# The third and fourth product of each slice change places in a fast-matrix-product attention kernel

## The chip, the cores and the metric

The kernel runs on one core of one Trainium2 chip. The metric is device microseconds of one execution. The median of the shown runs of the kernel before is 2908.41 us.

## The reference

The input `x` holds 128 graphs of 128 nodes with 768 features, and `adj` one 128x128 matrix for each graph. One pre-normalised attention layer with 12 heads of 64 is computed:

```python
h = relu(layernorm(x))                       # over the 768 features, eps 1e-5
q, k, v = split_heads(h @ Wq + bq), split_heads(h @ Wk + bk), split_heads(h @ Wv + bv)
scores = q @ k^T / sqrt(64) + beta * adj     # adj is shared by the 12 heads
scores = where(adj > 0, scores, -9e15)
out = x + merge_heads(softmax(scores) @ v)
```

The biases of the three projections are zero in the inputs, and everything is float32.

## The kernel before

**Tiling.** Four graphs make one group, and there are 32 groups (`G`). The features lie on the partitions, in three pairs of 128-row blocks. The projections of a group are done in three slices: `qk0` (queries and keys of heads 0 to 5), `v` (all values), `qk1` (queries and keys of heads 6 to 11). Seen in blocks, each slice is a 2x3 by 3x3 matrix product. It is computed with 15 block products instead of 18, each of a sum of blocks of the activations (names A.. and S..) with a sum of blocks of the weights (names B.. and T..). The table `PRODUCTS` holds them in the order in which they are issued. The first `qk0` slice, of group 0, is done plainly with 18 products, so 95 slices go by the table. The last slice of all has an order of its own, `LAST`, which is a list of positions in the table.

**Banks.** Each row of the table names a chain, a to d. The products of one chain are added up in one PSUM bank, one after another. After each product the running sum in the bank is added to, or taken from, the output blocks that the row lists: the first time that an output block is met it is written (by ScalarE in the qk slices, line 352, by VectorE in the v slices, line 342), and later it is updated by VectorE (line 356 or 347). This reading of a bank is called its drain here. The next product of the chain may write the bank only when its drain has ended. A chain takes a bank from the list of free ones at its first product and gives it back after its last:

```python
first = n == mine[0]
if first:
    banks[chain] = take()
```

There are eight banks, and the list is first in, first out.

**Scores.** With `SC_AT = 1`, the scores of six heads follow the second product of a slice, in the 31 `qk0` slices of groups 1 to 31, the 31 `v` slices of the same groups and the `qk1` slice of group 0. They take six banks at once, three pairs in the order `3u, 3u+2, 3u+1`:

```python
ps = {(oc, i): take() for oc in order for i in range(2)}
...
e = es[G, oc, i] = work.tile(...)
taken[0] = nc.vector.scalar_tensor_tensor(e, ps[oc, i]..., SCORE_CAP * ISCALE, biasT[G], ...)   # L381
give(ps[oc, i])
nc.scalar.activation(e, e, AF.Exp, scale=1.0 / ISCALE)                                          # L384
```

With the two banks that chains c and a hold by then, all eight are in use. The next bank that anybody takes is the one that the first line 381 has read. Line 377 is the matmul of the scores, line 410 that of probabilities with values (after products 5, 8 and 11), line 331 that of the block products. `issue_after(added[G].ins)` in `transposes` keeps the transposes for the next group (line 279, in `to_hT`) behind the latest VectorE drain traced so far. `HT_AT` places them after products 0 to 4 and 9 of the `qk1` slice. `stats` (line 227) reads the `x` tiles that `load_x` (line 152) brings in for a later group.

**Order of the work.** The Tile scheduler puts the instructions of each engine in an order at compile time, by the order of the program and by when it reckons each to be ready. VectorE, ScalarE and the DMA queue of SyncE then run their lists in that order.

Of the kernel before, what the change touches and what calls it, by code (L numbers as in the profile page):

```python
# [31 lines left out]
def kernel(  # L32
# [33 lines left out]
PRODUCTS = (  # L66
    ("S9", "T9", "c", (((1, 1), -1),)),
    ("A10", "T12", "a", (((1, 0), -1),)),
    ("S10", "T10", "b", (((1, 0), 1),)),
    ("S2", "T2", "c", (((0, 1), -1),)),  # L70
    ("S8", "B12", "d", (((1, 1), -1), ((1, 2), 1))),
    ("S6", "T6", "a", (((0, 0), -1),)),
    ("S3", "B01", "c", (((0, 2), -1),)),
# [694 lines left out]
```

## Time and profile before

| what | value |
| --- | --- |
| median of 5 runs | 2908.41 us (2906.64 to 2909.24) |
| the profiled execution's own time | 2904.81 us |
| its span | 2903.0 us |
| PE busy | 2878.8 us, 99% of the span |
| weight loads (PEld) busy | 2015.1 us, 69% |
| VectorE (DVE) busy | 1988.1 us, 68% |
| ScalarE (ACT) busy | 806.9 us, 28% |
| GpSimd (POOL) busy | 376.0 us, 13% |
| granted TensorE clock | 0.999 of full speed |

A line of a timeline gives the start and the length in us, the engine, the source line, the operation, what it writes and reads, and how many instructions were merged. At its end stand, in brackets, the idle time of the engine just before it and what ended that idle time. The weights of a product are loaded by PEld just ahead of its matmuls, so a wait of a product shows in front of its first weight load.

### The profile page before, as it was taken

How to read it: one execution, taken by the hardware profiler on the slowest of the kernel's cores; microseconds unless marked ns; L12 is line 12 of the kernel's file. 1: busy time of each engine (PE TensorE's matmuls, PEld its weight loads, DVE VectorE, ACT ScalarE, POOL GpSimd, SP SyncE). 2: the span in 40 equal slices, each digit the busy share in tenths (PEclk: the TensorE clock that was granted, in tenths of full speed). 3: DMA queues.
4: the chain of work that ended last, by engine and by line, in shares of the span. 5: the costliest groups of instructions: out<-in, count | busy, mean ns of one | idle time of the engine just before them, and what ended most of it. 6: DMA issues, size and time to landing. Idle time of an engine off the chain costs nothing.

```text
span 2903.0 us, 81884 instructions
## 1 busy us (share of the span) xinstructions
PE 2878.8 (99%) x35526; PEld 2015.1 (69%) x35526; DVE 1988.1 (68%) x5143; ACT 806.9 (28%) x1751; POOL 376.0 (13%) x307
## 2 busy tenths in 40 slices
PE   8999999999999999999999999999999999999998
PEld 6666777666667666766667666677666676666766
DVE  7876667666676666767667776667666677666765
ACT  2432322223222222223232232322223222322221
POOL 1111111111111111111111111111111111111110
PEclk9999999999999999999999999999999999999999
DMA  6312122221222111221112212122221222111211
GB/s 165 78 52 57 44 61 70 56 60 41 56 70 63 53 45 52 71 67 51 54 44 67 71 52 58 43 61 70 56 60 42 56 70 63 52 49 45 67 42 38
DMA packets 358622, 172.22 MB, mean 59 GB/s; under 512 B 84464, under 2 KB 358128, under 8 KB 358256
## 3 DMA queue, kind: packets, MB, share of 16 engines
q1 hardware_dynamic: 355392, 166.14, 21.2%
q8 instruction: 280, 4.59, 0.7%
q10 hardware_dynamic: 2864, 0.79, 0.1%
q14 instruction: 86, 0.70, 0.1%
HBM read 116.53 MB, written 50.33 MB: 57 GB/s over the span
## 4 chain that ended last, share of the span: by engine, by line
PE 83%; issue 8%; DVE 5%; POOL 2%; DMA 2%; SPq 1%; ACT 0%; ACTq 0%; POOLq 0%; DVEq 0%
PE bank L331 71%; PE bank L377 5%; PE bank L410 5%; DMA x<-in_x_dram 2%; PE bank L481 1%; DVE S L285 1%; POOL rstd L261 1%; POOL xo L415 1%; DVE qk L356 1%; DVE st L227 1%; DVE A L279 1%; SPq L152 0%; DVE o L393 0%; DVE e L381 0%; SPq L416 0%
## 5 line engine op out<-in xcount | busy, mean ns | idle before, releaser
L331 PE MATMUL bank<-S,qk_T 128*64 128x256 f32 x7056 | 822.6, 380 | 5.1 <-DVE e L381 3.1
L331 PEld LDWEIGHTS bank<-S,qk_T 128*64 128x64 f32 x7056 | 502.4, 137 | 263.8 <-DVE e L381 8.2
L356 DVE TENSOR_TENSOR qk<-qk,bank 128x512 f32<-128x512 f32 x630 | 430.1, 683 | 343.1 <-PE bank L331 342.9
L352 ACT ACTIVATE qk<-bank,bqk 128x256 f32<-128x256 f32 x756 | 313.4, 471 | 990.8 <-PE bank L331 848.3
L331 PE MATMUL bank<-S,qk_B 128*64 128x256 f32 x4032 | 478.3, 379 | 1.1 <-DVE qk L356 0.9
L331 PE MATMUL bank<-A,qk_T 128*64 128x256 f32 x4032 | 478.5, 379 | 0.4 <-DVE qk L356 0.4
L415 POOL TENSOR_TENSOR xo<-xo,o 128x512 f32<-128x512 f32 x189 | 256.1, 1355 | 1604.6 <-DVE o L393 993.1
L331 PE MATMUL bank<-v_T,S 128*64 128x256 f32 x3584 | 422.7, 380 | 0.0
L384 ACT ACTIVATE e<-e 128x512 f32<-128x512 f32 x378 | 227.6, 631 | 665.6 <-DVE e L381 664.8
L347 DVE TENSOR_TENSOR v<-v,bank 128x512 f32<-128x512 f32 x320 | 220.1, 688 | 264.8 <-PE bank L331 264.7
L331 PEld LDWEIGHTS bank<-A,qk_T 128*64 128x64 f32 x4032 | 283.6, 137 | 137.6 <-DVE qk L356 0.5
L331 PEld LDWEIGHTS bank<-S,qk_B 128*64 128x64 f32 x4032 | 277.9, 137 | 129.8 <-DVE qk L356 1.7
L331 PEld LDWEIGHTS bank<-v_T,S 128*64 128x64 f32 x3584 | 252.1, 137 | 126.5 <-issue 5.7
L272 ACT ACTIVATE x<-x,shift,rstd 128x192 f32<-128x192 f32 x512 | 228.1, 534 | 343.8 <-POOL shift L263 343.8
L331 PE MATMUL bank<-v_B,S 128*64 128x256 f32 x2048 | 244.7, 380 | 0.0
L381 DVE SCALAR_TENSOR_TENSOR e<-bank,biasT 128x512 f32<-128x512 f32 x378 | 231.4, 682 | 16.7 <-PE bank L377 16.7
L331 PE MATMUL bank<-v_T,A 128*64 128x256 f32 x2048 | 238.3, 379 | 0.0
L342 DVE TENSOR_TENSOR v<-bv_b,bank 128x512 f32<-128x512 f32 x192 | 131.9, 687 | 146.4 <-PE bank L331 146.4
L410 PEld LDWEIGHTS bank<-v,e 128*64 128x64 f32 x6048 | 208.5, 138 | 27.4
L279 DVE STREAM_TRANSPOSE A<-x 128x256 f32<-128x256 f32 x384 | 215.8, 614 | 7.6 <-ACT x L272 7.4
L227 DVE BATCH_NORM_STATS2 st<-x 128x6 f32<-128x192 f32 x512 | 160.9, 349 | 74.7 <-DMA x<-in_x_dram 74.2
L410 PE MATMUL bank<-v,e 128*64 128x65 f32 x6048 | 208.2, 221 | 0.0
(80 smaller groups left out, 1729.9 us busy)
## 6 DMA issues: line engine op xcount, KB each, us to landing
x<-in_x_dram SPq DMA_DIRECT2D x504, 96.0 KB, 2.5
xo<-in_x_dram SPq DMA_DIRECT2D x189, 256.0 KB, 2.8
out_dram<-xo SPq DMA_DIRECT2D x189, 256.0 KB, 2.2
adj<-in_adj_dram SPq DMA_DIRECT2D x128, 64.0 KB, 2.4
qk_T<-in_L_gnn_Wq_dram SPq DMA_DIRECT2D x10, 128.0 KB, 3.4
qk_T<-in_L_gnn_Wk_dram SPq DMA_DIRECT2D x10, 128.0 KB, 3.3
v_T<-in_L_gnn_Wv_dram SPq DMA_DIRECT2D x5, 256.0 KB, 5.9
qk_B<-in_L_gnn_Wq_dram SPq DMA_DIRECT2D x8, 128.0 KB, 3.4
```

The source lines that it names most:

```text
L227: nc.vector.bn_stats(st[G][:, g * NB + b, :], xg[G, g][:, b, :])
L272: nc.scalar.activation(t, t, AF.Relu, bias=shift[G, n], scale=rstd[G, n])
L279: last = nc.vector.transpose(t[:, :, g * N:(g + 1) * N].rearrange("p c (b i) -> p c b i", i=SQ), src)
L331: nc.tensor.matmul(p[q:q + HD, i, :], lhs[:, q:q + HD], rhs, start=(first and i == 0 and c == 0), stop=(c == 1), skip_group_check=True)
L347: added[G] = nc.vector.tensor_tensor(o, o, got, ALU.add if sign > 0 else ALU.subtract)
L352: nc.scalar.activation(t[:, i, :], p[:, i, :], AF.Identity, bias=bqk[:, i, oc:oc + 1], scale=float(sign))
L356: added[G] = nc.vector.tensor_tensor(t, t, p, ALU.add if sign > 0 else ALU.subtract)
L377: nc.tensor.matmul(ps[oc, i][k:k + HD, g * N:(g + 1) * N], t[r, 1, at][:, k:k + HD], t[r, 0, at], start=True, stop=True)
L381: taken[0] = nc.vector.scalar_tensor_tensor(e, ps[oc, i].rearrange("p (g n) -> p g n", g=GRP), SCORE_CAP * ISCALE, biasT[G], op0=ALU.min, ...
L384: nc.scalar.activation(e, e, AF.Exp, scale=1.0 / ISCALE)
L410: nc.tensor.matmul(pa[q:q + HD, 2 * g + i, :], es[G, oc, i][:, 2 * r + g, q:q + HD], vt[G, "v", r, h // 4][:, 4 * g + h % 4, :], start=Tru ...
L415: nc.gpsimd.tensor_add(t, t, o.rearrange("p a (b j) d -> p (a b) (j d)", j=2))
```

## The change

Two neighbouring rows of the table change places. Product S2·T2 of chain c now comes third, straight behind the scores where there are any, and product S10·T10, which opens chain b, comes fourth. All 95 slices that use the table are affected, also those without scores, and so is `LAST`, since it names positions. No instruction is added or removed.

```diff
     ("S9", "T9", "c", (((1, 1), -1),)),
     ("A10", "T12", "a", (((1, 0), -1),)),
+    ("S2", "T2", "c", (((0, 1), -1),)),
     ("S10", "T10", "b", (((1, 0), 1),)),
-    ("S2", "T2", "c", (((0, 1), -1),)),
     ("S8", "B12", "d", (((1, 1), -1), ((1, 2), 1))),
     ("S6", "T6", "a", (((0, 0), -1),)),
     ("S3", "B01", "c", (((0, 2), -1),)),
```

## The prediction

> **What bounds the kernel now.** I read the page first. PE is busy for 99% of the span, so only PE's pauses can be won, and only work on PE or a new pause can be lost.
>
> ```profile
> PE 2878.8 (99%) x35526; PEld 2015.1 (69%) x35526; DVE 1988.1 (68%) x5143; ACT 806.9 (28%) x1751; POOL 376.0 (13%) x307
> ```
>
> Second, the waits, asked for all engines; these three rows are the pauses in front of the weight loads of block products (us in total, times, longest):
>
> ```profile
> PEld bank L331 <- DVE e L381: 8.2, 22, 1.1
> PEld bank L331 <- issue: 7.7, 44, 0.3
> PEld bank L331 <- DVE qk L356: 6.5, 10, 1.4
> ```
>
> The first row is what the change aims at: the product behind the scores waits until line 381 has read a bank of the scores. It stands 22 times, for 8.2 us in all.
>
> Third, the timeline of PEld, to see how much of these 8.2 us is really a wait. A quiet place (a v slice) and a disturbed one (the qk0 slice with the longest wait):
>
> ```profile
> 233.88 2.61 PEld L377 LDWEIGHTS bank<-qk 64*64 64x64 f32 x96 [0.39 <-issue]
> 236.66 3.22 PEld L331 LDWEIGHTS bank<-v_T,S 128*64 128x64 f32 x32 [0.17 <-issue]
> ...
> 828.98 2.61 PEld L377 LDWEIGHTS bank<-qk 64*64 64x64 f32 x96 [0.38 <-issue]
> 832.69 3.22 PEld L331 LDWEIGHTS bank<-S,qk_T 128*64 128x64 f32 x32 [1.09 <-DVE e L381]
> ```
>
> A gap of 0.17 us follows the scores in every slice, also where nothing is waited for. It stays. What can go is 1.09 - 0.17 = 0.92 us in the worst slice. The `x32` shows that S10 and S2, 16 records each, follow the scores at once.
>
> Fourth, why line 381 is late there, from VectorE's timeline:
>
> ```profile
> 827.92 0.35 DVE L227 BATCH_NORM_STATS2 st<-x 128x6 f32<-128x192 f32 x1
> 830.91 1.14 DVE L227 BATCH_NORM_STATS2 st<-x 128x6 f32<-128x192 f32 x4 [2.63 <-DMA x<-in_x_dram]
> 831.96 3.66 DVE L381 SCALAR_TENSOR_TENSOR e<-bank,biasT 128x512 f32<-128x512 f32 x6
> ```
>
> VectorE stands in its queue for 2.63 us at statistics of a later group whose `x` has not landed, and line 381 is behind them.
>
> **The change part by part.**
>
> *The wait behind the scores goes.* S2 adds to chain c's bank, which no score holds. Subtracting the 0.17 us from each of the 22 gaps: 8.2 - 22 x 0.17 = 4.46 us. All 22 lie in qk0 slices. The 31 v slices, and the qk1 slice of group 0, show only the 0.17 us. S10 comes one product later, which is 1.73 us (weight loads of successive products start at 169.28, 171.01 and 172.73 us). The longest excess was 0.92 us, so S10 finds its bank free with 0.8 us to spare. S8 takes the second bank of the scores, which is read 0.61 us (3.66/6) after the first and asked for 3.45 us after S2: free too. Against the profiled execution's own time: 2904.81 - 4.46 = 2900.35 us.
>
> *What more a usual run holds.* The profiled execution took 2904.81 us, 1.81 us more than its span, and is 3.60 us below the median. From one scores stage of the qk0 slices to the next a period is 89.40 us where nothing is disturbed (2176.43 to 2265.83 us). The 30 periods from 115.13 to 2803.67 us sum to 2688.54 us, that is 6.54 us above 30 x 89.40. Nearly all of the 4.46 us is in this, the rest is mostly the third wait row. What varies within an execution is thus waits on late `x`, 4.46/6.54 = 0.68 of them of the kind that goes. Whether the 3.60 us are more of the same no view shows. The bounds are 0 and 3.60 us; I take the share, 0.68 x 3.60 = 2.45 us, since these waits are the nearest thing in the trace that varies. Sum: 4.46 + 2.45 = 6.9 us.
>
> *Chain c is entered again after one product instead of two.* Where scores stand between (62 slices and one more), 2.78 us of them lie between A10 and S2, so c is long drained. In 32 slices, nearly all qk1, nothing lies between but A10. The same place in ScalarE's and PEld's timelines:
>
> ```profile
> 171.44 0.84 ACT L352 ACTIVATE qk<-bank,bqk 128x256 f32<-128x256 f32 x2 [4.22 <-PE bank L331]
> ```
>
> ```profile
> 169.28 1.66 PEld L331 LDWEIGHTS bank<-S,qk_T 128*64 128x64 f32 x16
> 171.01 1.65 PEld L331 LDWEIGHTS bank<-A,qk_T 128*64 128x64 f32 x16
> 172.73 3.38 PEld L331 LDWEIGHTS bank<-S,qk_T 128*64 128x64 f32 x32
> ```
>
> S9 is drained from 171.44 to 172.28 us; the third product's first load starts at 172.73. So 0.45 us are left over, and A10 is the cover. ScalarE had been idle for some 4 us before that drain in every qk1 slice of groups 1 to 30, so this does not scatter. The v slice of group 0 has a VectorE drain there (49.44 to 50.13 us, with the third product due near 50.7), also in time. Cost 0. From above it is bounded by a drain wholly in the open, 0.88 us (0.84 and 0.04 of start) x 32 = 28 us; a gain is excluded, since chain c waits nowhere there today.
>
> The Trainium skill speaks against this step: Perfetto Trace Analysis, section Optimizing Tensor Performance, Matmuls, says that independent matmul groups should rotate through different PSUM banks, so that evacuating one overlaps the matmuls of the next. Going on in the open bank shortens that rotation from three products to two; by the rule alone the sum would lean to a loss in the 32 slices, by the row it is nothing, and no run here shows it yet.
>
> *Drains that move.* In qk0 slices S2's drain is ScalarE's, queued behind six Exp. At 1102 us these end at 1105.65 and the drain at 1107.67 us; chain c's next product S3 starts at 1109.88 us. S2 ending earlier cannot delay that. S10's drain there starts at 1106.17 us, behind the six line 381 and a biasT copy, although S10 was done near 1103.9; ended 1.73 us later it is still before 1106.17. Chain b is next used by S7, four slots later in the new table after S10. Cost 0, hidden by those products; without that cover it would be one drain, 0.69 us.
>
> *VectorE in the qk1 slices.* S10's drain comes 1.73 us later, and the transposes change sides of it. Today, at 1067 us:
>
> ```profile
> 1067.52 2.24 DVE L279 STREAM_TRANSPOSE A<-x 128x256 f32<-128x256 f32 x4
> 1072.16 0.69 DVE L356 TENSOR_TENSOR qk<-qk,bank 128x512 f32<-128x512 f32 x1 [2.41 <-PE bank L331]
> 1072.77 2.24 DVE L279 STREAM_TRANSPOSE A<-x 128x256 f32<-128x256 f32 x4
> 1075.55 0.69 DVE L356 TENSOR_TENSOR qk<-qk,bank 128x512 f32<-128x512 f32 x1 [0.54 <-PE bank L331]
> ```
>
> After the change, S2 leaves no VectorE drain in position 2, so A11's pair may go before S10's drain, into the 2.41 us of idle. S10's drain starts at 1073.89, A02's pair (half of 2.24) ends at about 1075.6, and S8's drain, due at 1075.55, is 0.1 us late. Nobody on PE waits for it soon: chain d comes back at position 8, four products after S8, with an attention step between. Cost 0, from 0 to the price in the third rival below. The DMA queue of SyncE gets no new order from the source, since loads sit at positions 2, 5, 6 and 8 as before; how the scheduler lays them out I cannot see, and it is part of the range.
>
> Total: 2908.41 - 6.9 = **2901.5 us**, 0.24% less.
>
> **The rivals.**
>
> 1. *Only what the profile shows goes.* The 3.60 us are something fixed, such as time outside the span, and stay: 2908.41 - 4.46 = 2903.9 us. For it speaks that no view shows them.
>
> 2. *The wait only moves.* S10 meets the same late line 381. That needs an excess over 1.73 us; of the 22 the largest is 0.92. It would give 2908.4 us.
>
> 3. *Slower: VectorE falls behind in qk1.* If the scheduler keeps all four transposes behind S10's drain, they end at 1073.89 + 0.61 + 2.24 = 1076.74 us, and S8's drain is 1.19 us late. Late VectorE work at the end of qk1 already stops PE (third wait row, ten times). In 15 of the 30 periods VectorE shows no slack, as they exceed 89.40 us; 15 x 1.19 - 4.5 = 13.4 us, so 2921.8 us. It decides from (5.8 + 4.5)/31 = 0.33 us of lost PE time per group. Against it: the order of the program puts A11's pair first.
>
> 4. *Slower: chain c's drain in qk1 is late.* Half of the bound of 28 us would be 14 us, net of 4.5 it gives 2917.9 us. It needs ScalarE 0.45 us later than it is in any group shown.
>
> **How the numbers follow.** About 0.2% (5.8 us, so 2902.6 and 2914.2 us) is what a measurement of this kernel can tell from no change. Chances: forecast 0.45, rival 1 0.27, rival 2 0.08, rival 3 0.12, rival 4 0.08. The forecast lies 1.1 us below the mark, so I count 0.40 of it as faster and 0.06 of rival 1, in case more goes than I think: faster 0.46. Rivals 3 and 4 make slower 0.20, the rest is within: 0.34. The range starts where all 3.60 us and the 2.1 us of other waits in the periods go as well (2908.4 - 4.5 - 3.6 - 2.1 = 2898.2) and reaches past no change to 2911, so that it leaves out most of rivals 3 and 4 and little else. The forecast's own range is 2898 to 2904 us.
>
> **What would show it.** The row of PEld waiting for DVE e at line 331 falls from 22 to nearly none, while 0.17 us of issue stands behind all 63 score stages. In VectorE's timeline of v slices line 342 comes ahead of line 347 behind the six line 381. In qk1, six transposes stand in a row before the first line 356, and no row of PE waiting for ACT qk at line 352 grows. The 30 periods shrink from 2688.5 towards 2684 us. It is wrong if qk1 shows PE waiting for line 352 or for line 356 oftener, or if the waits for line 381 come back in front of S10.

## The result and the profile after

The kernel after takes 2901.41 us (median of 24 runs, 2899.66 to 2902.45), the kernel before 2907.64 us (median of 44 runs, 2904.79 to 2910.06). The ratio is 0.9978, with a 95% interval of 0.9972 to 0.9983: 6.2 us, or 0.22%, faster. The prediction had 2901.5 us. The profiled execution of after took 2900.81 us, 4.0 us less than that of before; its span is 2898.7 us, 4.3 us less.

The first row of the page after: PE has the same work and the same busy time as before in a shorter span.

```profile
PE 2878.8 (99%) x35526; PEld 2017.3 (70%) x35526; DVE 1984.3 (68%) x5143; ACT 803.7 (28%) x1751; POOL 375.2 (13%) x307
```

The waits after (us in total, times, longest), in front of weight loads of block products:

```profile
PEld bank L331 <- issue: 8.9, 51, 0.3
PEld bank L331 <- DVE qk L356: 4.2, 7, 1.4
PEld bank L331 <- ACT e L384: 2.6, 15, 0.2
```

The row for line 381, 8.2 us before, is gone. The third row is new by name only: each of its 15 gaps is the 0.17 us that follow the scores in any case. Not foreseen is the second row, which fell from 6.5 to 4.2 us (2.8 us of it lie in group 0, before and after). PEld's timeline after, the same group as the worst wait shown of before:

```profile
829.38 2.61 PEld L377 LDWEIGHTS bank<-qk 64*64 64x64 f32 x96 [0.39 <-issue]
832.17 3.22 PEld L331 LDWEIGHTS bank<-S,qk_T 128*64 128x64 f32 x32 [0.17 <-issue]
```

And VectorE's timeline beside it:

```profile
828.29 0.35 DVE L227 BATCH_NORM_STATS2 st<-x 128x6 f32<-128x192 f32 x1
830.64 1.14 DVE L227 BATCH_NORM_STATS2 st<-x 128x6 f32<-128x192 f32 x4 [2.00 <-DMA x<-in_x_dram]
831.70 3.66 DVE L381 SCALAR_TENSOR_TENSOR e<-bank,biasT 128x512 f32<-128x512 f32 x6
```

VectorE still stands 2.00 us for a late `x`, so that line 381 starts 2.32 us after the first weight load of the scores. In a quiet v slice of before that was 1.14 us (1041.18 to 1042.32 us). PE no longer notices: S2 goes on with chain c's bank.

The 30 periods from one qk0 scores stage to the next sum to 2682.53 us (116.81 to 2799.34 us), against 2688.54 us before, and 30 undisturbed ones of 89.40 us are 2682.0 us. Of 6.54 us of waits 0.53 us are left. That is 6.0 us, of which the profile of after shows only 4.3 in the span, because its start was 1.7 us slower (the first v slice begins at 49.17 us, before at 47.45 us). That start is no part of the change. The first two products of the kernel (16 weight loads) took

```profile
15.32 3.32 PEld L481 LDWEIGHTS bank<-A,qk_T 128*128 128x128 f32 x16 [1.98 <-DVE A L279]
```

in the profile of before, and in that of after

```profile
15.55 4.81 PEld L481 LDWEIGHTS bank<-A,qk_T 128*128 128x128 f32 x16 [1.98 <-DVE A L279]
```

Of the twelve profiled executions in this document six took 3.32 us here and six 4.77 to 5.01 us, and the kernel before has one of each. In one of the slow ones (the swap outside the qk0 slices, below) the granted clock reads 0.50 from 17 to 20 us, while these products run. In after the trace has no clock record before 18.6 us, so that the same cause is likely there and not shown.

### The profile page after: what moved, and what is told of

It reads as the page before. It is cut to its first block, busy times and chain, and to the rows that moved or that the text cites. A ratio compares the mean times of both kernels' runs of the same rounds, so it can differ in the third digit from the quotient of the medians.

```text
span 2898.7 us, 81826 instructions
## 1 busy us (share of the span) xinstructions
PE 2878.8 (99%) x35526; PEld 2017.3 (70%) x35526; DVE 1984.3 (68%) x5143; ACT 803.7 (28%) x1751; POOL 375.2 (13%) x307
## 4 chain that ended last, share of the span: by engine, by line
PE 97%; DVE 1%; issue 1%; DMA 0%; ACT 0%; POOL 0%; SPq 0%; POOLq 0%; DVEq 0%
PE bank L331 83%; PE bank L377 6%; PE bank L410 6%; PE bank L481 1%; DMA x<-in_x_dram 0%; DVE A L279 0%; DVE qk L356 0%; DVE S L285 0%; DVE e L381 0%; ACT x L272 0%; PE bank L238 0%; PE bank L254 0%; DMA qk_T<-in_L_gnn_Wq_dram 0%; POOL rstd L261 0%; DVE qk_T L207 0%
## 5 line engine op out<-in xcount | busy, mean ns | idle before, releaser
L331 PEld LDWEIGHTS bank<-v_T,A 128*64 128x64 f32 x2048 | 147.5, 137 | 73.9
```

The costliest lines, as they stand in the source:

```text
L331: nc.tensor.matmul(p[q:q + HD, i, :], lhs[:, q:q + HD], rhs, start=(first and i == 0 and c == 0), stop=(c == 1), skip_group_check=True)
```

## The experiments

The theory: the time gone is S10's wait for the first bank of the scores in the qk0 slices, and that bank is late because VectorE stands at statistics of a late `x`. The rival: the swap also changed the lists of VectorE and of the DMA queue, and the gain came from there.

**The swap in the qk0 slices alone.** Order (0, 1, 3, 2, 4 to 14) over the table of before:

```diff
-            slice_of(G, "qk0", todo)
+            slice_of(G, "qk0", todo, SWAPPED)
```

> The two products change places in the 31 qk0 slices only; v and qk1 slices keep the order of before. Theory (the time gone is the wait of S10 for line 381 in the qk0 slices, and nothing else): the row PEld <- DVE e at L331 is empty or nearly so, and the time is that of after, 2901 to 2903 us, some 5 to 6 us under before. Rival (the gain comes from another order of transfers and VectorE work that the swap in the v and qk1 slices brought along): within 1.5 us of before, 2906 to 2908 us. If both have a part, between the two: the waits for line 356 near the end of qk1 stay at some 2 us as before, and the time is about 1.5 us above after.

Measured: 2902.4 us against 2908.2 us for before beside it, ratio 0.9979 (0.9970 to 0.9989). Line 381's row is gone, the periods stand 1.79 us over 2682.0 us, and VectorE's waits for `x` stay at 72.2 us (74.2 us before, and 74.9 us in a second profile of before). So the wait behind the scores, taken away by itself, is worth about 5.8 us, and what is left over in the periods are the waits for line 356.

**The swap everywhere else.**

```diff
-        slice_of(G, "v", todo)
+        slice_of(G, "v", todo, SWAPPED)
-            slice_of(G, "qk1", todo)
+            slice_of(G, "qk1", todo, SWAPPED)
-LAST = (0, 1, 2, 3, 5,
+LAST = (0, 1, 3, 2, 5,
```

> The counterpart: the two products change places in the v and qk1 slices and in the last slice only; the qk0 slices keep the order of before. Theory: the waits for line 381 stay, 4 to 7 us over some 20 qk0 stages, and the time is that of before, 2906 to 2908 us. Rival (transfer order): most of the gain, 2902 to 2904 us, with the line 381 waits shrunk because x lands earlier. With both: some 1.5 us under before, from fewer waits for line 356.

Measured: 2903.83 us, ratio 0.9986 (0.9977 to 0.9995), which is what the rival expected. The waits of this run:

```profile
PEld bank L331 <- DVE qk L356: 5.9, 11, 1.4
PEld bank L331 <- DVE e L381: 5.0, 15, 0.9
DVE st L227 <- DMA x<-in_x_dram: 56.7, 62, 2.5
```

Beyond the 0.17 us gaps line 381's waits fell from 4.46 to 5.0 - 15 x 0.17 = 2.45 us, and the periods from 6.54 to 3.81 us over 2682.0 us, although no product behind the scores of a qk0 slice was moved. VectorE's waits for `x` fell to 56.7 us, about as in after (54.9 us). So both have a part: the time is 4.4 us under before (1.5 to 6.7 us by the interval). The two parts overlap: 5.8 + 4.4 is more than the 6.2 us of both together.

**Statistics behind the scores, on both kernels.**

```diff
-                    then(11 + g, lambda g=g: stats(G + 1, g))
+                    then(11 + g, lambda g=g: behind_scores(stats, G + 1, g))
```

> The kernel before, with the statistics of later groups (line 227, groups 2 on) kept behind the last line 381 on VectorE, so that a late x can no longer hold line 381 up; the order of the products is untouched. Theory (line 381 is late because VectorE stands at statistics whose x has not landed): the waits for line 381 vanish without the swap, and most of the gain comes, 2900 to 2904 us. The waits for line 356 at the end of qk1 go too, as the statistics were in front of those as well; but 16 statistics, some 4.5 us of VectorE work, now stand behind the scores and can make the drains of S10 and S8 late, which could give back some us. Rival (line 381 is late for another reason, such as the sums or drains in front of it): the waits stay at 4 to 7 us and the time is 2906 to 2909 us.

> The kernel after, with the statistics kept behind the last line 381 in the same way. Theory: after has almost no removable wait left in its 30 periods (2682.53 us against 30 x 89.40 = 2682.0), so this is the same within 1 us, 2900.5 to 2902.5 us. If waits in unprofiled runs are larger than in the profiled one, it may win 1 us more. Rival (statistics behind the scores make the drains of S10 and S8 late and PE waits for them): 2903 to 2910 us.

Measured: 2898.56 us on the kernel before (ratio 0.9969, 0.9958 to 0.9980) and 2898.58 us on the kernel after (0.9966, 0.9954 to 0.9978). In both, the 30 periods sum to 2682.0 us: nothing is left to win there. The late statistics were the cause, and with the cause gone no worth of the swap shows. The second expectation, the same as after within 1 us, was missed by 2 us on the good side. That is hardly a second gain of the statistics: of the 2.3 us between the two profiled spans (2898.7 and 2896.4 us) 0.53 us lie in the periods and 1.7 us in the start told above. The feared late drains did not show: line 356's row is 2.8 us in both, all of it in group 0.

**What the other slices had to do with it.** In the kernel before, the scheduler had put statistics of the second graph (x_1, the fifth and sixth of a group's 16) into the second attention step of qk1. VectorE's timeline of before shows it, lines 389, 391 and 393 being that step's normalising:

```profile
1084.88 0.15 DVE L389 TENSOR_SCALAR sm<-bank 128x4 f32<-128x4 f32 x1
1085.91 0.36 DVE L227 BATCH_NORM_STATS2 st<-x 128x6 f32<-128x192 f32 x1 [0.88 <-DMA x<-in_x_dram]
1086.19 0.16 DVE L391 RECIPROCAL rs<-sm 128x4 f32<-128x4 f32 x1
...
1086.31 0.35 DVE L227 BATCH_NORM_STATS2 st<-x 128x6 f32<-128x192 f32 x1
1086.58 0.41 DVE L393 TENSOR_TENSOR o<-bank,rs 128x256 f32<-128x256 f32 x1
```

In the kernel after, the step comes through unbroken and the wait stands behind it:

```profile
1083.51 0.15 DVE L389 TENSOR_SCALAR sm<-bank 128x4 f32<-128x4 f32 x1
1083.70 0.18 DVE L391 RECIPROCAL rs<-sm 128x4 f32<-128x4 f32 x1
1083.80 0.13 DVE L399 TENSOR_TENSOR seen<-seen,sm 128x4 f32<-128x4 f32 x1
1083.91 0.42 DVE L393 TENSOR_TENSOR o<-bank,rs 128x256 f32<-128x256 f32 x1
1084.25 0.15 DVE L399 TENSOR_TENSOR seen<-seen,rs 128x4 f32<-128x4 f32 x1
1085.50 0.36 DVE L227 BATCH_NORM_STATS2 st<-x 128x6 f32<-128x192 f32 x1 [1.09 <-DMA x<-in_x_dram]
```

The step's result goes to GpSimd and then to a store, and loads of the next `x` stand behind that store in SyncE's queue. In SyncE's timeline of before that store and the loads behind it are:

```profile
1082.91 0.40 SPq L416 DMA_DIRECT2D out_dram<-xo  x1
...
1088.37 0.40 SPq L416 DMA_DIRECT2D out_dram<-xo  x1
1088.88 0.94 SPq L152 DMA_DIRECT2D x<-in_x_dram  x2
```

The second store comes 5.46 us after the first. In the kernel after it is 4.17 us (1081.54 to 1085.71 us). The other groups show the same: over 30 of them the median is 5.6 us in both executions of before and with the swap in the qk0 slices alone, and 4.18 us in after and with the swap everywhere else. To try that chain, only x_1's statistics were held back in the kernel before:

```diff
-                    then(11 + g, lambda g=g: stats(G + 1, g))
+                    then(11 + g, lambda g=g: (behind_scores if g == 1 else lambda f, *v: f(*v))(stats, G + 1, g))
```

> The kernel before, with only the second graph's statistics (x_1) kept behind line 381; those of the other graphs stay ahead of it, and PE's, ScalarE's and GpSimd's lists are the same as before. Theory (part of the gain comes from VectorE's order in qk1: statistics of x_1 whose transfer is late stand inside the normalising of the second attention step, so that its result, its store and the x loads queued behind that store on SyncE come late, and with them the statistics ahead of line 381): the waits of VectorE for x fall from 74 towards 55 us or below, the waits for line 381 to about half (2 to 3 us over the 0.17 us gaps), the time to 2902 to 2905 us, as in the run that swaps in v and qk1 only. Rival (the statistics there do no harm; the run with v and qk1 swapped was faster for another reason): the waits for line 381 stay at 4 us or more, and the time at 2906 to 2909 us.

Measured: 2899.9 us, ratio 0.9971 (0.9960 to 0.9982), periods 2682.01 us, line 381's row 0.5 us in 3 gaps (all 0.17 us), VectorE's waits for `x` 40.9 us, and the second store 4.18 us after the first. More than expected: with x_1's four statistics, of 16, out of the way, nothing is left of the waits behind the scores. Two things changed at once here. The stores come earlier, the third too (4.74 us ahead of the scores in the median of 30 groups, 3.93 us in after, 3.43 us in before), and four statistics fewer, 1.1 us of VectorE's work, stand ahead of line 381. What each of them is worth by itself is not shown.

**The first bank made later still.** Three more passes over the first bank of the scores, ahead of its line 381, in both kernels:

```diff
+                [nc.vector.tensor_scalar(ps[oc, i], ps[oc, i], 1.0, None, op0=ALU.mult) for _ in range(0 if i or oc != order[0] else 3)]
                 e = es[G, oc, i] = work.tile(...)
```

> The kernel before, with three more VectorE passes (times 1.0, in place) over the first bank of each scores stage ahead of its line 381, so that this bank comes free some 3 x 0.61 = 1.83 us later in all 63 stages; the result does not change. Theory (the product behind the scores waits for that bank): in a quiet stage the first line 381 ends near 1.83 us after the scores' first weight load and S10's load is due at 2.78 us, so 0.95 us are spare and 0.88 us of wait appear in each of 63 stages: 55 us, plus the waits already there, 2960 to 2970 us. Rival (PE does not hang on that bank, only on VectorE's load as a whole): 2908 to 2920 us.

> The kernel after with the same three extra passes. Theory: S10 asks for the bank one product, 1.73 us, later, so 0.95 + 1.73 - 1.83 = 0.85 us are still spare in a quiet stage; only stages where x is late by more than that wait: 2901 to 2906 us, against 2960 to 2970 us for the kernel before with the same passes. Rival (the wait moves to S10 or to a later drain): over 2915 us.

Measured: before 3029.91 us (ratio 1.0423, 1.0405 to 1.0440), after 2911.37 us (1.0013, 1.0003 to 1.0023). The waits, first in the kernel before and then in the kernel after with these passes:

```profile
PEld bank L331 <- DVE e L381: 117.5, 63, 3.7
```

```profile
PEld bank L331 <- DVE e L381: 9.3, 12, 1.5
```

The sign and the contrast are as the theory says: all 63 stages wait in the one, and in the other only some qk0 stages and no v stage. The sizes were too small. A pass costs 0.73 us in a row of three (2.20 us together), not 0.61, so a quiet stage waits 1.30 us (a gap of 1.47 us less 0.17). That is 82 us, and the disturbed stages bring the row to 107 us over the 0.17 us gaps, 102 us more than in before. The rest is a slower PE clock, told at the end: 13 stretches of some 1.7 us each, about 22 us. In the kernel after, S10's spare time was 0.85 by the expectation and 0.95 + 1.73 - 2.20 = 0.48 us as measured, so the qk0 stages with a late `x` ran out of it.

**Half the cover for chain c's drain.** In the kernel after, order (0, 2, 1, 3 to 14) in qk1:

```diff
-            slice_of(G, "qk1", todo)
+            slice_of(G, "qk1", todo, BARE if G else range(15))
```

> The kernel after, with second and third product exchanged in the qk1 slices of groups 1 to 30. By the scheduler's order S2 then stands inside A10, after half of A10's matmuls, so that chain c is entered again with half a product (0.86 us) between instead of a whole one. Theory (0.45 us were spare with a whole product): 0.86 - 0.45 = 0.41 us of wait for line 352 in each of 30 slices, 12 us: 2912 to 2916 us. Rival (the bank can be entered while the drain runs, or the drain is shorter than it looks): no wait, 2901 to 2903 us.

Measured: 2910.21 us, ratio to before 1.0007 (0.9998 to 1.0017), so some 8 to 9 us are lost against after. The group at 1069 us, PEld and then ScalarE:

```profile
1067.13 1.65 PEld L331 LDWEIGHTS bank<-S,qk_T 128*64 128x64 f32 x16
1068.86 0.79 PEld L331 LDWEIGHTS bank<-A,qk_T 128*64 128x64 f32 x8
1070.18 1.49 PEld L331 LDWEIGHTS bank<-S,qk_T 128*64 128x64 f32 x16 [0.53 <-ACT qk L352]
```

```profile
1069.29 0.84 ACT L352 ACTIVATE qk<-bank,bqk 128x256 f32<-128x256 f32 x2 [4.16 <-PE bank L331]
```

S2's load starts 0.05 us after the drain's end (1070.13 to 1070.18 us). It waits in every qk1 slice of groups 1 to 30, but costs less than expected: the periods lengthen by (9.90 - 0.53)/30 = 0.31 us each, not 0.41. Weight loads run some 0.2 us ahead of their matmuls, and a part of a late load is taken from that lead.

**The transposes behind S10's drain.** In the kernel after:

```diff
-HT_AT = {"A01": 0, "A00": 1, "A11": 2, "A02": 3, "A10": 4, "A12": 9}
+HT_AT = {"A01": 0, "A00": 1, "A11": 3, "A02": 3, "A10": 4, "A12": 9}
```

> The kernel after, with A11's transposes placed after the fourth product instead of the third, so that four transposes stand behind S10's drain on VectorE and S8's drain in qk1 starts some 1.1 us late. Theory (VectorE catches up before the end of qk1): the same as after within 2 us, 2900 to 2903 us. The prediction's third rival (VectorE late in qk1 stops PE at line 356): up to 18 us more, 2910 to 2920 us.

Measured: 2900.68 us, ratio 0.9976 (0.9965 to 0.9986), the same as after. VectorE's timeline shows the lateness as meant:

```profile
1071.05 0.69 DVE L356 TENSOR_TENSOR qk<-qk,bank 128x512 f32<-128x512 f32 x1 [4.14 <-PE bank L331]
1071.65 2.23 DVE L279 STREAM_TRANSPOSE A<-x 128x256 f32<-128x256 f32 x4
1073.80 0.65 DVE L356 TENSOR_TENSOR qk<-qk,bank 128x512 f32<-128x512 f32 x1
```

S8's drain starts 2.75 us after S10's and not 1.7. The periods stand only 0.18 us over 2682.0 us, so VectorE makes up for it. This edit, too, moved other work: VectorE's waits for `x` are 29.1 us here, 54.9 us in after.

**The kernel before once more.**

> The kernel before once more, for its profile alone: how much the waits for line 381 scatter from execution to execution. Theory (the 3.6 us by which the median lies above the first profile are more of the same waits): an execution near 2908 us shows some 6 to 7 us of wait behind the scores (over the 0.17 us gaps) and 9 to 10 us over 30 x 89.40 us. Rival (the 3.6 us lie elsewhere): about 4.5 and 6.5 us again at 2908 us.

Measured: 2908.82 us, 4.01 us above the first profile. Its rows:

```profile
PEld bank L331 <- DVE e L381: 8.5, 19, 1.4
PEld bank L331 <- DVE qk L356: 8.5, 12, 1.4
```

Behind the scores it waits 8.5 - 19 x 0.17 = 5.3 us, 0.8 us more than the first; line 356's row is 2.0 us longer; the periods are 2690.88 us, 2.3 us longer. The other 1.7 us lie ahead of them, in the start: the first two products took 4.77 us of PEld, in the first profile 3.32 us. Neither theory is right: the 3.6 us are partly waits, partly the start.

## Why the prediction was right, and which step was not

- *The wait behind the scores goes, 4.46 us.* Right. None of the 63 stages waits after, and the qk0 swap alone gains 5.8 us.
- *What more a usual run holds, 2.45 us.* Mis-sized. This took 0.68 of the 3.60 us as more waits of the kind that goes. The second profile of before shows 0.8 of 4.0 us, so by the same working the term is about 0.7 us. Of the 4.0 us 1.7 are the start, which is no wait of this kind.
- *Drains that move, and VectorE in the qk1 slices, cost 0.* The failed step, and what hid the fault in the other. The text looked only for a loss, and left the scheduler's order to the range. The swap in the v and qk1 slices gave x_1's statistics another place on VectorE, and this is worth 4.4 us by itself. On top of the qk0 swap it is small: 1.79 us of waits left in the periods fall to 0.53 us, 1.3 us. This is from one profile of each, and the two medians, 2902.4 and 2901.41 us, are not clear of each other. So 4.5 + 0.7 + 1.3 = 6.5 us are close to the 6.2 us measured, and the 2.45 us stood in for the last two. That the total agreed within 0.1 us is partly luck: 6.9 us were forecast and 6.2 us came, from a median of before that was 0.8 us lower over 44 runs than over the five (2907.64 and 2908.41 us).
- *Chain c entered again after one product, cost 0.* Right, with the spare time as worked out: in the kernel after S9 is drained at 1068.12 us (1067.28 + 0.84) and the third product's first load starts at 1068.57 us, 0.45 us later. The Trainium skill's rule to rotate banks (Perfetto Trace Analysis, Optimizing Tensor Performance, Matmuls) holds in kind, as half a product of cover costs 0.31 us a slice; with a whole product it costs nothing here.
- *Rival 1 (2903.9 us)* lies outside the measured range. *Rival 2* needed a wait over 1.73 us; no stage of after shows one. *Rival 3* is refuted twice: six transposes stand ahead of S10's drain, and with four put behind it the time is the same (with other work moved too). *Rival 4* would need a later ScalarE, and there is none.
- *What would show it:* the periods came to 2682.53 us, better than the 2684 us named. In the v slices line 342 does come ahead of line 347 behind the six line 381 (1044.60 us), and PE's waits for line 352 stay at one of 0.3 us.

## What to carry to other kernels

A wait on a buffer can be taken away at the waiting side (work that needs no buffer goes first) or at the late side. Here the late side did at least as well: the trouble was a few statistics of a later group, put ahead of urgent work while their data was still under way, and holding them back gives 2898.6 to 2899.9 us without touching the products. Where a scheduler lays out the lists, a swap also moves instructions elsewhere, so a change is tried in its parts before its gain is put down to its name, and an estimate allows for a gain from such moves as well as a loss. And before a difference of 2 us between two profiles is explained, the start is compared: here it alone differs by 1.7 us between executions of one kernel.

## What the runs showed of the hardware

PE's granted clock fell to half after some pauses and not after others. In the kernel before with the three passes this came 13 times behind the scores of qk0 slices, after pauses of PE of 1.94 to 3.42 us, and each time for 3.41 us; after other pauses of up to 2.38 us, and after those of the v slices (1.2 to 1.3 us), it did not. One case, in windows of 2 us after a pause of 2.92 us on PE (the third column from the right is the clock):

```profile
1060.00:1062.00 2.00, 1.62 (x12) 1.08 (x14) 2.00 (x4) 1.58 (x3) 0.00 (x0) 0.83 0.00 0
1062.00:1064.00 2.00, 2.00 (x12) 1.14 (x10) 2.00 (x5) 2.00 (x4) 0.53 (x1) 0.50 0.00 0
1064.00:1066.00 2.00, 2.00 (x18) 1.19 (x16) 1.30 (x2) 0.82 (x3) 0.00 (x0) 0.82 0.00 0
```

Two products took 5.36 us there instead of 3.67. By the gaps in front of the weight loads, one of 2.31 us at 309.29 us was followed by a clock of 0.65 over the next 3.7 us, one of 2.62 us at 1155.22 us by a clock of 1.00. The Trainium skill (TensorE: Matmul & The Clock Gate, Part 1) puts the fall after an idle window of about 3.4 us that runs free of the program. The trace agrees with the free running: the 13 stretches start whole multiples of 3.413 us apart. For the length it differs: pauses of 2 to 3 us were enough here, and the measurement decides. The lesson for this kernel: a pause of 2 us can cost 1.7 us more than itself, and one of 1.2 us, the longest of PE behind the scores in the two executions of before, shows no such cost.
